# A perceiver block on one core: the pace of the gathers, the passage from the first mixture to cross-attention, and the order of five tiles

## The chip, the cores and the metric

The kernel runs as one program on one core of a Trainium2 chip. A core has five engines, each with an instruction queue of its own: TensorE (PE; its weight loads are listed apart as PEld), VectorE (DVE), ScalarE (ACT), GpSimd (POOL) and SyncE (SP, which here only issues DMAs). An engine works through its queue in order; where an instruction needs another engine's result, it waits on a semaphore, and everything behind it in that queue waits too. Transfers run on 16 DMA engines beside all this.

The metric is the device time of one execution in microseconds (us), as the median of several runs. All data are float32.

## The reference

Two layers over `x` of shape (16, 64, 256), that is 1024 tokens, with a context of 1601 rows of 256 for each of the 16 batches. Each step adds to `x`:

```python
    x = x + _L0_xattn_ref(ctx_1024, ctx_1024, _layernorm(x, axis=-1), mask_BxS2_if0, ...)
    x = x + _L0_attn_ref(_layernorm(x, axis=-1), ...)
    x = x + _L0_ffn_ref(_layernorm(x, axis=-1), ...)
    x = x + _L1_xattn_ref(_layernorm(x, axis=-1), ctx_1024, ...)
    x = x + _L1_attn_ref(_layernorm(x, axis=-1), ...)
    x = x + _L1_ffn_ref(_layernorm(x, axis=-1), ...)
    return x
```

- Layer 0, deformable attention: every query computes 5 sample positions for each of 16 heads from itself; at each position the keys and values of two neighbouring context rows are gathered and mixed, and a softmax over the 5 samples weighs them.
- Layer 0, attention: within a batch's 64 tokens, with normed queries and keys and a sigmoid instead of a softmax.
- Layer 0, mixture: 8 experts of width 512 with gelu gates, the best 2 per token.
- Layer 1, cross-attention: 16 heads of 64 over the context, 77 text rows and 1524 image rows with a softmax each, the two results added.
- Layer 1, state space: a convolution of 4 taps, then a recurrence over 64 tokens with 16 states, gated by a silu.
- Layer 1, mixture: 32 experts of width 128, the best 4 per token, and a shared expert of width 512.

## The kernel before

**Tiles and stages.** The 1024 tokens are 8 tiles of 128 (two batches each), held in `x4`. The work runs in this order:

1. *Keys and values* (`keys_values`, 113 steps `s`): context rows are loaded (`cx`), transposed on TensorE, multiplied by `wkv`, copied by ScalarE into `kv` and written to a table `tab` in DRAM for each tile of queries. Beside it DVE computes the sample positions, and `texts` prepares the text rows for cross-attention.
2. *Gathers and attends.* The sampled rows are fetched from the tables by `gather(k)`: DVE copies ten indices (`ig`), GpSimd issues ten indirect DMAs of 128 rows each (L446). Two gathers make a unit of four heads of one tile, and `attend(i)` (three pieces: DVE, one Exp on ScalarE, DVE) turns it into a part of `cv`. There are 32 units, four per tile, 64 gathers.
3. *Layer 0's rest for tiles 0 to 2* (`ND0 = 3`): `attention`, then `middle`, the mixture with all 8 experts computed on all tokens; the weights of an expert are three tiles of 512 KB in the tag `w` with four buffers. For tile 3 there is `attention` alone (`late`).
4. *Cross-attention* (`Cross`), 128 steps `n` (16 batches by 8 pairs of heads). A step multiplies the transposed context rows `cT` by the folded query `qf` (24 products `st`), takes a maximum on DVE (`mp`, `xmx`), subtracts it and exponentiates (`pt`), and one step later multiplies by the rows themselves (`cn`, L1096).
5. *Layer 0's rest for tiles 3 to 7*, beside cross-attention: `attention` and `middle` with a table `tb0`, which only route; then `slots` (which token stands in which block), `gelus` (17 blocks of 128 gathered tokens, each with one expert) and `combine` (the results gathered back, `yk`).
6. *State space and the second routing* beside the rest of cross-attention, and the second mixture at the end (`dense`, `Blocks`), beside the state space of the last two tiles.

**What sets the order.** The order on PE, DVE and ACT is the program's own (`manual_schedule`): generators yield pieces, and the loops place them. Gathers and attends are placed by `tick(us)`: it advances a clock of the program's own, by an amount in us that the program states for each piece of work, and issues a gather if `APART` (16.0; `APART_X`, 12.0, once `cr` exists) of it have passed since the last one and fewer than four units are open, and a piece of an attend if `AFTER` (42.0) have passed since its second gather. Nothing in it is measured at run time. GpSimd's queue holds the gathers and the memsets (`qbd`, `pt`, the column of ones in `cn`) in the order in which they are issued.

**The places that the change touches.**

- `tick`, L1551: the pace of the gathers.
- `mid`, L1579, called once in each step `s` from 60 on: one piece of `mids`, that is of `attention` or `middle` for tiles 0 to 2. `mids[0]` waits in the program's order until enough units are attended.
- From L1613: behind the keys and values, the loop `while mids`, which runs what is left of these pieces with no other work beside it; before it `qbd` gets its memset on GpSimd (L1619).
- `Cross.begin`, L1204: the first queries (`queries`, three parts; their weights `wq` are two loads of 512 KB), the turn of the context rows of batch 0 (`turn`), the loads for batch 1, the text part of batch 0, the first fold. `fold(n + 1)` at L1160 computes the next step's `qf`.
- From L1646: the side work of stage 5 as one chain, tile 3 singly, then 4 and 5, then 6 and 7 in pairs. `cr.step(side, side, side, side)` takes one piece of it at four places of a step, and `next(side, None)` a fifth. It must be done by `cr.n = 42`; what is left is run at once (`drain(side)`).
- `Blocks.fetch`, L1436, and `Blocks.down`, L1464: a block's weights are loaded for the expert whose number SP reads from `ev4`, which DVE copies (L1452); each block's result `yb` is copied out of PSUM by DVE and ScalarE in turn (`copy(n, ...)`).

## Time and profile before

| what | value |
|---|---|
| median of 3 runs | 3019.71 us (3013.13 to 3023.61) |
| the profiled execution | 3017.05 us, span from first to last instruction 3014.8 us |
| granted TensorE clock, mean | 0.974 |
| PE busy | 2826.2 us (94%), 17734 instructions |
| PEld busy | 2354.7 us (78%) |
| DVE busy | 1618.4 us (54%) |
| ACT busy | 1033.6 us (34%) |
| POOL busy | 819.7 us (27%), of it the gathers' indirect DMAs 613.2 us (640 of 958 ns) |
| HBM | 235.79 MB read, 74.62 MB written, 103 GB/s over the span |

The spans count from the first instruction. A group's idle time is that of its engine just ahead of the group's instructions, with what ended it; for an engine that isn't the bottleneck it costs nothing. Float32 products appear as two records each in the trace, so 9751 instructions of PE in the program are 17734 records. The granted clock is the share of full speed that the chip allows TensorE in a window; a busy time at a clock of 0.84 holds 0.84 of the work that the same busy time holds at full clock.

The page's 40 slices show in which stages PE is not full (tenths of each slice of 75 us; the PE clock and the share of the DMA engines below it):

```profile
PE   8999999967999998889979999999999999998699
DVE  3332133244666675553236766577544676655756
POOL 0655545556676730000010110011000020001623
PEclk9999999988999998899989999999999999999999
DMA  7666856636122221125521111122011021004853
```

The low digits of PE stand in four places: the first slice, slices 9 and 10 (600 to 750 us, the way from the keys and values to cross-attention), slices 16 to 18 and 21 (1125 to 1350 us and about 1500 us, tiles 3 to 7), and slices 37 and 38 (2700 to 2850 us, the start of the second mixture). GpSimd's digits of 5 to 7 between 75 and 1125 us are the gathers.

### The profile page before, as it was taken

The page shows a single profiled execution, that of the slowest core. Times are in us where ns is not written, and L with a number is a line of the kernel's source. Part 1 is how long each engine was busy: PE and PEld are TensorE (multiplying, and loading weights), DVE is VectorE, ACT ScalarE, POOL GpSimd, SP SyncE. Part 2 cuts the span into 40 slices and gives each one's busy share as a digit, 9 for nine tenths or more (in the row PEclk, how much of TensorE's full clock was granted, in tenths as well). Part 3 has the DMA queues.
Part 4 walks back from the last instruction along what each step waited for, and adds up shares of the span by engine and source line. Part 5 has one row for each costly group of instructions (what it writes and reads, how often), then busy time and mean ns, then how long its engine had stood idle before and what let it go on. Part 6 is the DMA issues. An engine that isn't in the chain of part 4 may idle for free.

```text
span 3014.8 us, 46081 instructions
## 1 busy us (share of the span) xinstructions
PE 2826.2 (94%) x17734; PEld 2354.7 (78%) x17734; DVE 1618.4 (54%) x4134; ACT 1033.6 (34%) x2375; POOL 819.7 (27%) x923
## 2 busy tenths in 40 slices
PE   8999999967999998889979999999999999998699
PEld 4554446656898997689969999899999999995587
DVE  3332133244666675553236766577544676655756
ACT  3433444323223223324323333343232443222431
POOL 0655545556676730000010110011000020001623
PEclk9999999988999998899989999999999999999999
DMA  7666856636122221125521111122011021004853
GB/s 231 177 194 213 252 167 179 196 110 189 34 64 56 71 56 48 36 96 182 188 68 55 60 60 55 35 75 70 17 47 58 29 88 62 8 1 128 242 150 112
DMA packets 324291, 313.43 MB, mean 104 GB/s; under 512 B 57941, under 2 KB 275321, under 8 KB 323561
## 3 DMA queue, kind: packets, MB, share of 16 engines
q1 hardware_dynamic: 171577, 212.52, 22.1%
q10 hardware_dynamic: 126928, 63.06, 7.3%
q0 software_dynamic: 25568, 34.91, 5.4%
q8 instruction: 141, 2.31, 0.3%
q14 instruction: 77, 0.63, 0.1%
HBM read 235.79 MB, written 74.62 MB: 103 GB/s over the span
## 4 chain that ended last, share of the span: by engine, by line
PE 82%; DVE 8%; DMA 4%; ACT 3%; issue 1%; POOL 0%; ACTq 0%; SPq 0%; DVEq 0%; POOLq 0%
PE st L88 35%; PE mm L1096 21%; PE mm L88 16%; PE mm L153 5%; PE mm L1052 2%; PE mm L1082 1%; DVE hs L1337 1%; DVE mp L1127 1%; PE mm L1021 1%; DMA w<-in_gate 1%; DMA wd<-in_down1T 1%; PE mm L1146 1%; DMA yk<-y0d,sli 1%; POOL g L446 0%; ACT pt L1168 0%
## 5 line engine op out<-in xcount | busy, mean ns | idle before, releaser
L1096 PE MATMUL mm<-cn,pt 128*128 128x257 f32 (+1 forms) x3072 | 745.0, 386 | 0.5 <-ACT cT L82 0.5
L88 PE MATMUL st<-qf,cT 128*128 128x128 f32 x6144 | 740.6, 278 | 0.9 <-ACT qf L1055 0.9
L446 POOL DMA_INDIRECT g<-tab,ig x640 | 613.2, 958 | 467.6 <-DVE ig L444 183.7
L88 PEld LDWEIGHTS st<-qf,cT 128*128 128x128 f32 x6144 | 722.2, 194 | 5.5 <-ACT qf L1055 1.7
L1096 PEld LDWEIGHTS mm<-cn,pt 128*128 128x128 f32 (+1 forms) x3072 | 557.1, 191 | 84.1 <-ACT cT L82 0.9
L88 PE MATMUL st<-wkv,cxt 128*128 128x512 f32 (+1 forms) x832 | 378.1, 599 | 2.8 <-ACT cxt L415 2.8
L1127 DVE TENSOR_REDUCE mp<-st 128x128 f32<-128x512 f32 x384 | 260.2, 686 | 208.4 <-PE st L88 208.1
L1167 DVE TENSOR_TENSOR pt<-st,mc 128x512 f32<-128x512 f32 (+1 forms) x384 | 224.0, 638 | 153.7 <-ACT mc L1158 153.7
L88 PEld LDWEIGHTS st<-wkv,cxt 128*128 128x128 f32 (+1 forms) x832 | 150.2, 189 | 160.7 <-issue 157.0
L1168 ACT ACTIVATE pt<-pt 128x512 f32<-128x512 f32 (+1 forms) x384 | 208.0, 588 | 50.3 <-DVE pt L1167 50.1
L399 ACT COPY kv<-st 128x512 f32<-128x512 f32 (+1 forms) x208 | 121.5, 586 | 199.9 <-PE st L88 198.8
L1158 ACT COPY mc<-mm 128x128 f32<-128x128 f32 x128 | 33.9, 265 | 394.2 <-PE mm L1156 393.7
L1105 ACT COPY ot<-mm 128x256 f32<-128x256 f32 x128 | 47.5, 371 | 336.1 <-PE mm L153 336.1
L957 POOL MEMSET cn<- 128x12 f32 x16 | 1.9, 122 | 522.0 <-PE mm L1096 512.2
L1443 POOL DMA_INDIRECT xb<-xnd,row x55 | 58.4, 1062 | 290.1 <-PE mm L1082 218.2
L1148 DVE TENSOR_REDUCE xmx<-mm 128x1 f32<-128x128 f32 x128 | 37.3, 291 | 186.1 <-PE mm L1146 186.1
L1343 POOL TENSOR_TENSOR mn<-mn,hc 128x512 f32<-128x512 f32 x64 | 82.0, 1281 | 169.4 <-DVE hc L1342 164.5
L1072 ACT COPY yt<-mm 128x64 f32<-128x64 f32 x128 | 27.2, 212 | 253.8 <-PE mm L88 253.8
L88 PE MATMUL mm<-xt,w 128*128 128x256 f32 (+1 forms) x512 | 98.5, 348 | 6.9 <-DMA w<-in_gate 5.2
L88 PEld LDWEIGHTS mm<-xt,w 128*128 128x128 f32 x512 | 86.4, 210 | 23.3 <-issue 9.6
L153 PEld LDWEIGHTS mm<-ident,cx 128*128 128x128 f32 (+1 forms) x416 | 52.9, 145 | 40.8 <-issue 28.5
L1337 DVE TENSOR_TENSOR_SCAN hs<-da,db 128x512 f32<-128x512 f32 x64 | 80.1, 1252 | 6.9 <-DVE db L1335 0.5
(466 smaller groups left out, 3884.0 us busy)
## 6 DMA issues: line engine op xcount, KB each, us to landing
tab<-kv ACTq DMA_DIRECT2D x48, 1024.0 KB
w<-in_gate SPq DMA_DIRECT2D x66, 512.0 KB
cx<-in_ctx SPq DMA_DIRECT2D x48, 512.0 KB
cn<-in_ctx SPq DMA_DIRECT2D x16, 1408.0 KB
w<-in_lin SPq DMA_DIRECT2D x33, 512.0 KB
wk<-in_xwkiT SPq DMA_DIRECT2D x32, 512.0 KB
wg<-in_guT SPq DMA_DIRECT2D x55, 256.0 KB
g<-tab,ig POOLq DMA_INDIRECT x640
```

The costliest lines, as they stand in the source:

```text
L88: nc.tensor.matmul(o, lhsT=l, rhs=r, start=i == 0, stop=i == len(pairs) - 1)
L153: nc.tensor.transpose(t[:ncol, i, :rows], b, ident[:rows, :rows])
L399: nc.scalar.copy(kv[:w, :, c, :], pk[:w].rearrange("p (h e) -> p h e", h=H0))
L446: nc.gpsimd.indirect_dma_start(out=gf[:, (half * n + s) * 4 * HD0 : (half * n + s + 1) * 4 * HD0], out_offset=None, in_=tables[j], in_offs ...
L1052: nc.tensor.matmul(pf[:, k * P : (k + 1) * P], lhsT=w[:, hp % 4, k * P : (k + 1) * P], rhs=rhs, start=True, stop=True)
L1096: nc.tensor.matmul(po, lhsT=pt[:w, c, :], rhs=cn[:w, c, :], start=c == 0, stop=c == NCH - 1)
L1127: nc.vector.tensor_reduce(mp_[:, i, :], s.rearrange("p c n -> p n c"), AX.X, ALU.max)
L1167: nc.vector.tensor_tensor(o, st[i][:, :m, :], mc.to_broadcast([P, m, P]), ALU.subtract)
L1168: nc.scalar.activation(o, o, AF.Exp)
L1337: nc.vector.tensor_tensor_scan(hs.rearrange("p c n -> p (c n)"), da.rearrange("p c n -> p (c n)"), db.rearrange("p c n -> p (c n)"), 0.0, ...
L1343: nc.gpsimd.tensor_tensor(y, y, hc, ALU.add)
L1443: nc.gpsimd.indirect_dma_start(out=x, out_offset=None, in_=xnd, in_offset=bass.IndirectOffsetOnAxis(ap=tb.row[:, i : i + 1], axis=0))
```

## The change

The gathers are 12.0 apart throughout. `mid` is called twice per step while `s < 94`. The first queries are placed between the last pieces of the mixture, with their weights in the mixture's own buffers `w`; `ahead` turns the context rows and folds steps 0 and 1 before the mixture's pool closes, and the text part of batch 0 goes into cross step 0. `fold` works two steps ahead, with a third buffer of `qf`, which moves to the pool `xc`. Tiles 3 to 7 are taken singly, in two rows with buffers of their own (`Row`; one buffer for each tag, `y` in that of `ct` and `sg` in that of `gt0`), one piece from each row by turns, and `slots` gives an empty piece after each of its own. In the second mixture the results of blocks with a number of `E1` or more are all copied by ScalarE, and the numbers of their experts are copied into `evs` in `slots`.

```diff
-APART, APART_X, AFTER = 16.0, 12.0, 42.0
+APART, AFTER = 12.0, 42.0
...
             nc.vector.tensor_copy(self.expert, pe[:1, : nb - b0])
+            self.evs = []
+            if self.own:
+                for q in range(0, nb - b0, 4):
+                    m = min(4, nb - b0 - q)
+                    self.evs.append(mk(rp, [1, 4], f"ev{q}", I32, bufs=1))
+                    nc.vector.tensor_copy(self.evs[-1][:, :m], self.expert[:, q : q + m])
...
+    class Row:
+
+        def __init__(self, pool, row):
+            self.pool, self.row = pool, row
+
+        def tile(self, shape, dtype, tag, name, bufs):
+            tag = {"y": "ct", "sg": "gt0"}.get(tag, tag)
+            return self.pool.tile(shape, dtype, tag=f"{tag}{self.row}", name=f"{name}{self.row}", bufs=bufs or 1)
+
-    def attention(t0, nt, lp, mw):
+    def attention(t0, nt, lp, mw, a0=0):
...
-        def queries(self, t, part):
+        def queries(self, t, part, pool=None):
...
+            tag, bufs = ("w", 4) if pool else ("wq", 2)
+            pool = pool or self.xp
...
-            qf = self.qf[n] = mk(self.xp, [P, KC, P], "qf", bufs=2)
+            qf = self.qf[n] = mk(self.xc, [P, KC, P], "qf", bufs=3)
...
-            self.fold(n + 1)
+            self.fold(n + 2)
...
+        def ahead(self, lp):
+
+            self.turn(0)
+            self.w[0, 0] = load(lp, "w", a["xwkiT"][:512, :].rearrange("(c p) d -> p c d", p=P), [P, 4, D], 4)
+            for n in range(2):
+                self.fold(n)
+
         def begin(self, xp):
+
             self.xp = xp
             self.text_loads(0)
             self.weights(0, 0)
-            yield
-            for part in range(3):
-                self.queries(0, part)
+            self.loads(1)
+
+            def pieces():
+                self.text(0, 0)
                 yield
-            self.turn(0)
-            self.loads(1)
-            yield
-            self.text(0, 0)
-            yield
-            self.text(0, 1)
-            self.text_turn(0, 0)
-            yield
-            self.text_turn(0, 1)
-            self.fold(0)
-            yield
+                self.text(0, 1)
+                self.text_turn(0, 0)
+                yield
+                self.text_turn(0, 1)
+                yield
+
+            return pieces()
...
-                    if r == 0:
-                        m = min(4, tb.nb - E1 - 4 * q)
-                        self.ev = mk(ep, [1, 4], "ev4", I32, bufs=3)
-                        nc.vector.tensor_copy(self.ev[:, :m], tb.expert[:, 4 * q : 4 * q + m])
-                    e = nc.sync.value_load(self.ev[0:1, r : r + 1], min_val=0, max_val=E1 - 1)
+                    e = nc.sync.value_load(tb.evs[q][0:1, r : r + 1], min_val=0, max_val=E1 - 1)
...
-            copy(n, self.y[:, self.m, :], po[:, :D])
+            copy(1 if i >= E1 else n, self.y[:, self.m, :], po[:, :D])
...
+    def taken_in_turns(gens):
+        while gens:
+            for z in list(gens):
+                if next(z, True) is None:
+                    yield
+                else:
+                    gens.remove(z)
+
+    def slower(gen):
+        for _ in gen:
+            yield
+            yield
...
-            pace["gather"] = now + (APART if cr is None else APART_X)
+            pace["gather"] = now + APART
...
             if lp:
                 mid()
+                if s < 94:
+                    mid()
...
+        i = 0
         while mids:
-            if attended() < mids[0][0]:
-                tick(2.4)
+            assert len(mids) == 1
+            if i in (3, 6):
+                cr.queries(0, i // 3 - 1, lp)
             mid()
+            i += 1
+        cr.queries(0, 2, lp)
         while attended() < 4 * (ND0 + 1):
             tick(2.4)
         drain(late)
+        cr.ahead(lp)
         slp.close()
...
-        drain(cr.begin(xp))
+        pieces = cr.begin(xp)
+        cr.step(pieces, pieces, None, pieces)
...
-        side = chain([middle(ND0, 1, lp, mw, tb0)]
-                     + [z for t0 in range(ND0 + 1, NPAIR, TG) for z in (attention(t0, TG, lp, mw), middle(t0, TG, lp, mw, tb0))]
-                     + [tb0.slots, lambda: gelus(lp, tb0), lambda: combine(lp, tb0, ND0, y0d, lambda t: None, 1)])
+        rows = [Row(lp, i) for i in range(TG)]
+        tiles = [[middle(ND0, 1, rows[0], mw, tb0)], []]
+        for t in range(ND0 + 1, NPAIR):
+            i = (t - ND0) % TG
+            tiles[i] += [attention(t, 1, rows[i], mw, i), middle(t, 1, rows[i], mw, tb0)]
+        side = chain([taken_in_turns([chain(z) for z in tiles]), lambda: slower(tb0.slots()),
+                      lambda: gelus(lp, tb0), lambda: combine(lp, tb0, ND0, y0d, lambda t: None, 1)])
```

More of the change, by code (lines that the diff above doesn't have):

```diff
@@ L768, in attention @@
                 nc.vector.tensor_scalar(sg[r], ps[r, r], 1.0 / math.sqrt(D), -math.log(S), ALU.mult, ALU.add)
-                nc.scalar.activation(att[t][r, r], sg[r], AF.Sigmoid)
+                nc.scalar.activation(att[a0 + t][r, r], sg[r], AF.Sigmoid)
         yield
@@ L777, in attention @@
                     lhsT=qkv[:, t, 2 * D + e * P : 2 * D + (e + 1) * P],
-                    rhs=att[t], start=True, stop=True,
+                    rhs=att[a0 + t], start=True, stop=True,
                 )
@@ L992, in turn @@
                 nc.scalar.copy(ct[:, k, IMG:], ct[:, k, : NCH * P - IMG])
-        def queries(self, t, part):
+        def queries(self, t, part, pool=None):
             if t >= NPAIR:
                 return
+            tag, bufs = ("w", 4) if pool else ("wq", 2)
+            pool = pool or self.xp
             if part == 0:
-                self.xn[t] = normed([t], "q", self.xp)
+                self.xn[t] = normed([t], "q", pool)
             elif part == 1:
-                self.xn[t] = turned(self.xn[t], 1, "q", self.xp)
+                self.xn[t] = turned(self.xn[t], 1, "q", pool)
             else:
@@ L1005, in queries @@
                 for q4 in range(2):
-                    w = load(self.xp, "wq", a["xwq4"][q4].rearrange("k c p n -> p (k c) n"), [P, 4, D], 2)
+                    w = load(pool, tag, a["xwq4"][q4].rearrange("k c p n -> p (k c) n"), [P, 4, D], bufs)
                     pq = bank().rearrange("p (c n) -> p c n", c=4)
```

## The prediction

> **What bounds the kernel now.** I first read the windows of the trace, cut where the program changes stage (columns: window; its length; busy us and instructions of PE, PEld, DVE, ACT, POOL; granted clock; DMA share; GB/s).
>
> ```profile
> 0.00:589.80 589.80, 567.89 (x1923) 315.97 (x1924) 181.07 (x592) 246.31 (x466) 283.01 (x310) 0.99 0.67 199
> 589.80:762.50 172.70, 119.66 (x623) 101.86 (x622) 77.07 (x240) 55.85 (x110) 104.75 (x112) 0.84 0.53 156
> 762.50:1134.00 371.50, 363.39 (x2697) 333.35 (x2697) 252.97 (x648) 101.68 (x269) 233.41 (x248) 0.99 0.23 58
> 1134.00:1305.30 171.30, 143.20 (x891) 125.90 (x892) 96.08 (x328) 61.69 (x140) 0.12 (x1) 0.88 0.10 33
> 1305.30:1489.70 184.40, 175.10 (x1294) 162.89 (x1294) 61.62 (x154) 62.78 (x135) 15.28 (x17) 0.98 0.54 172
> 1489.70:1541.50 51.80, 33.70 (x243) 30.80 (x243) 13.06 (x31) 10.54 (x24) 11.44 (x17) 0.86 0.36 112
> 1541.50:2724.00 1182.50, 1176.62 (x8753) 1080.72 (x8752) 743.91 (x1675) 407.87 (x992) 67.79 (x108) 1.00 0.16 48
> 2724.00:3014.80 290.80, 246.60 (x1316) 203.23 (x1316) 192.62 (x469) 86.84 (x240) 103.91 (x111) 0.97 0.56 164
> ```
>
> TensorE is the bound almost everywhere, so the time to win is what a stage is longer than its TensorE work at full clock, estimated as length minus busy times clock: 172.7 - 119.7 x 0.84 = 72 us in stage 2 (the end of layer 0 behind the keys and values), 45, 13 and 23 us in stages 4 to 6 (tiles 3 to 7 beside cross-attention: attention and routing, expert blocks, the last of both), 52 us in stage 8 (the second mixture), and 6 to 28 us in each of the others. The waits of PE then say what ends the idle time, in stage 2 and in stage 4 (us in total, times, longest).
>
> ```profile
> PE mm L153 <- DVE qkv L103: 7.4, 2, 5.4
> PE mm L88 <- DMA wq<-in_xwq: 7.2, 1, 7.2
> PE mm L153 <- DVE cv L499: 6.2, 1, 6.2
> ```
> ```profile
> PE mm L153 <- DVE xn L103: 15.6, 4, 5.5
> PE mm L153 <- DVE qkv L103: 7.1, 2, 3.6
> PE mm L1146 <- DVE mp L1129: 5.7, 3, 2.7
> ```
>
> They are dependent chains (a norm, then its transpose), not a full engine: DVE is busy 45% and 56% there. Last I read GpSimd's timeline at the end of the keys and values, and the timelines of DVE and PE at the end of stage 6 (start, duration, instruction, idle before it).
>
> ```profile
> 595.00 0.94 POOL L446 DMA_INDIRECT g<-tab,ig  x1 [0.30 <-issue]
> 596.24 0.94 POOL L446 DMA_INDIRECT g<-tab,ig  x1 [0.30 <-issue]
> 597.23 1.80 POOL L1619 MEMSET qbd<- 128x2048 f32 x1
> ```
> ```profile
> 1537.95 0.48 DVE L702 SCALAR_TENSOR_TENSOR x<-yk,gk,x 128x256 f32<-128x256 f32 x1 [0.89 <-DMA yk<-y0d,sli]
> 1538.36 1.28 DVE L1127 TENSOR_REDUCE mp<-st 128x128 f32<-128x512 f32 x2
> ```
> ```profile
> 1540.95 0.47 PE L1146 MATMUL mm<-ident,mp 128*128 128x128 f32 x1 [17.18 <-DVE mp L1129]
> ```
>
> A gather's indirect DMAs start 1.25 us apart back to back, so one call of `gather` (ten) costs GpSimd 12.5 us. The memsets of `qbd` stand behind the gathers in the same queue. At the end of stage 6 the combination's ten gathered rows hold DVE, and PE waits 17.18 us behind them.
>
> **The change, part by part.** Counted in the built order of both kernels, TensorE's 9751 instructions stay; they only move. The sum is of waits.
>
> *Gathers 12 apart, two calls of `mid` per step.* In the order before, 13 of the 32 attends and 30 of the 64 gathers stand ahead of the end of the keys and values; in the order after, 23 and 52. Tiles 0 to 2 move with them: of stage 2's PE work (256 records of 128x128 at 3.57/32 = 0.112 us, about 230 of 128x256 at 0.217, the rest some 23 us; 102 us, which agrees with 119.7 x 0.84 = 101) only two experts of tile 2, the first queries, the turn of the context rows and two folds stay behind the last `wkv` product: 22 us. The 77 us that move go into a stage whose PE is 96% busy, so they lengthen it by 77 us and cost nothing net; their weights (25 MB) are as many bytes as before, and 144 MB by 762 us become 146 MB by some 740 us, at 197 GB/s, the rate of stage 1. With 10 us for waits in the denser stretch and 10 in the remainder, PE alone would reach the first cross product at 590 + 77 + 10 + 22 + 10 = 709 us instead of 762.5.
>
> *What is late next.* That is not when it will get there. GpSimd issues its first gather at 77.4 us; at 12 us of model time per 12.5 us of work it has no pause afterwards. In the changed order `qbd`'s memset stands behind 52 gathers, not 30: 77.4 + 52 x 12.5 = 727 us at the least, 733 with the mean of 12.3 us from a gather's first start to its last end plus 0.3 to the next, then 1.8 us of memset. ScalarE's first write to `qbd` (the queries' scaling, L1012) waits for that memset, and behind it on ScalarE stand the copies of `cT` and of `qf`, which PE needs for the first cross product. Before, that way took 762.5 - 748.7 = 13.8 us, of which the text's part (753.4 to 760.9) now goes into step 0: 6.3 us remain. The first cross product is at 733 + 1.8 + 6.3 = 741, 21.5 us earlier; the text's 3 us of PE come back in step 0. Gain 19 us; bounds: -15 (all 52 at the longest call's 13.0 + 0.3: 775, less the text) to 50 (were GpSimd not late: 709, less the text). I stay by the mean of the 64 calls.
>
> *Queries, loads and folds moved ahead.* The 7.2 us wait for `wq` goes: its two 512 KB loads now use the mixture's `w` buffers and stand in SP's queue behind the last expert loads, with the slack until 733 above them. Were GpSimd not late, they would cost up to that 7.2 again. One more 512 KB load (`xwkiT`) and the earlier `cn` load for batch 1 lie in the same slack. `fold` two ahead removes two waits of 0.5 us.
>
> *Tiles 3 to 7 in two rows.* The last attend now stands at cross step 14 instead of 27, so the side work starts there. It has 122 pieces instead of 90, five per step: attention and routing at steps 14 to 23 (before 27 to 32), slots to 28, expert blocks at 29 to 35, combination at 36 to 38, all under the limit of 42; before, the last blocks and the whole combination were run at once between steps 41 and 42. One tile's norm is half the DVE work of two, and each row has two gaps to finish in, some 5 us of cross PE work instead of 2.5. A row has one buffer per tag, and `y` shares that of `ct`; its pieces follow each other anyway, so that costs nothing while they are two gaps apart. So of stage 4's 45 us I keep 12 (a gap between the third and fifth call is only the last product, 1.7 us); stage 5's 13 become 13, since 2.5 blocks per step stay; of stage 6's 23 I keep 8, because ten row gathers at 1.9 us each still pass DVE within two steps. Gain 33 + 15 = 48; bounds 15 (below) and 70 (all but the blocks' 13).
>
> The price is on ScalarE: 28 more table loads (112 to 140), 1.283 us each by the trace's rows, 36 us, of which about 14 loads, 18 us, fall on these ten steps. A step lasts some 15.7 us there, ScalarE's own work is 62 us in the 171 us of stage 4, so they hide unless one stands ahead of `mc` (L1158), whose copy frees the banks; a load on that way at every second step would cost 5 x 1.3 = 7 us.
>
> [...]
>
> *Copies on ScalarE, expert numbers ahead of the stage.* In stage 8 they take twelve copies from DVE and move six more away:
>
> ```profile
> L84 DVE COPY yb<-mm 128x256 f32<-128x256 f32 x12 | 5.0, 420 | 1.6 <-PE mm L88 1.6
> ...
> L1452 DVE COPY ev<-evr 1x4 int32<-1x4 int32 (+1 forms) x6 | 3.9, 648 | 0.0
> ```
>
> That is 8.9 us of DVE, which is on the chain from 2759 to 2793 and by turns with loads of `wd` (5 to 7.6 us each) until 2857. I take half, 5 us; bounds 0 and 10.
>
> Sum: 19 + 48 + 5 = 72 us, from a profiled span of 3014.8 us (3017.1 with what lies around it). The median of the three runs is 3019.7, 2.7 us above that execution; I take the 72 from the median: 2947.8, say 2947.
>
> **The rivals.** *TensorE sets the pace up to cross-attention*, GpSimd is not late: 31 us more, 2916. For it speaks that PE's own work ends at 709; against it 520 DMAs at 1.25 us, a pace that no row undercuts. 0.08.
>
> *The rows gain little*: DVE's queue, not the tile's chain, is what PE waits for (`mp` L1129 is in the list above), and more small norms and table loads leave it so. Then 15 of the 48 remain: 2980. For it: a step's own DVE work is 7 us of 12.3, and the order puts a second row's pieces between. Against it: stage 7 has DVE 63% busy and PE at 1176.6 of 1182.5. 0.15.
>
> *The gathers slow each other and the change is slower*: ScalarE waits for `qbd` behind all 52, so the start of cross-attention goes with 520 times one DMA. It turns at 762.5 + 50 = 812.5 us, that is at 1.40 us each instead of 1.25; at 1.45 us the first cross product is at 840, 77 us late, and 77 - 50 = 27 us are lost: 3047. For it: single DMAs of 1.42 us instead of 0.94 do occur (589.5). Against it: the ten take 12.2 to 13.0 us in all 64 calls, also where DVE is 68% busy (stage 3). 0.05.
>
> [...]
>
> *The parts cancel or the order doesn't bind*, about 3018: 0.02.
>
> **How the numbers follow.** Forecast 0.70, with its own range 2920 to 2972; rivals 0.08, 0.15, 0.05, 0.02. The time is the forecast's. The range takes in the first two rivals: 2905 to 2985. Faster by over 0.3% (9 us, about what a measurement here can tell): 0.70 + 0.08 + 0.15 = 0.93; within: 0.02; slower: 0.05.
>
> **What would show it.** After: back-to-back gathers from 77 us with no pause, `qbd`'s memset at 727 to 740 us, and ScalarE's first `qbd` write idle until then. Right also: no wait of 17 us of PE on `mp`, `xn` and `qkv` waits under 8 us together, clock above 0.95 in the side steps. Wrong: the memset reached before 715, the first cross product after 765, or a stage from the last attend to step 42 with more than 50 us between its length and its PE work.

## The result, and the profile after

| | before | after |
|---|---|---|
| median | 3021.66 us (3013.13 to 3027.21, 4 runs) | 2978.70 us (2978.07 to 2980.21, 4 runs) |
| span of the profiled execution | 3014.8 us | 2976.4 us |
| granted TensorE clock, mean | 0.974 | 0.980 |
| first score product `st` of cross-attention | 762.5 us | 754.8 us |
| cross steps 1 / 14 / 42 / 127 (start of `xmx`) | 782.5 / 955.5 / 1541.5 / 2719.5 | 781.4 / 956.5 / 1505.3 / 2677.3 |

The ratio is 0.9863, 95% interval 0.9842 to 0.9885: 43 us faster by the medians, 38.4 by the two spans. The forecast was 72. By the steps of cross-attention, which exist in both kernels, the 38.4 us fall as follows: -1.0 up to step 14 (forecast: 19), 37.2 from step 14 to 42 (48), 6.0 from 42 to 127 (nothing), -3.8 from the last step to the end (5). A step is marked by its maximum `xmx` on VectorE; the steps' times in this text are read from those instructions' starts in the trace. The last stretch, from the last `xmx` to the end, is 295.3 us before and 299.1 after (the prediction's last window begins 4.5 us behind the last `xmx`).

The windows of the changed kernel, cut where its stages change (columns as in the prediction: window; length; busy us and instructions of PE, PEld, DVE, ACT, POOL; granted clock; DMA share; GB/s):

```profile
0.00:590.00 590.00, 548.46 (x1936) 323.38 (x1936) 245.16 (x786) 243.60 (x462) 387.26 (x413) 0.98 0.65 192
590.00:754.80 164.80, 132.97 (x588) 89.44 (x588) 54.38 (x168) 65.24 (x124) 126.50 (x132) 0.90 0.66 194
754.80:956.50 201.70, 189.46 (x1424) 174.57 (x1424) 133.56 (x340) 57.68 (x144) 114.26 (x124) 0.98 0.27 68
956.50:1155.70 199.20, 177.60 (x1186) 159.41 (x1183) 115.10 (x359) 90.90 (x194) 0.12 (x1) 0.93 0.11 33
1155.70:1227.20 71.50, 70.40 (x521) 64.47 (x520) 37.85 (x122) 20.48 (x48) 2.04 (x3) 0.98 0.17 54
1227.20:1422.00 194.80, 191.31 (x1423) 178.24 (x1422) 60.08 (x138) 72.80 (x153) 15.61 (x18) 1.00 0.58 182
1422.00:1505.30 83.30, 83.30 (x621) 76.50 (x620) 48.25 (x113) 32.75 (x73) 9.54 (x17) 1.00 0.25 71
1505.30:2677.30 1172.00, 1167.65 (x8714) 1073.36 (x8714) 736.45 (x1657) 397.80 (x974) 67.58 (x107) 1.00 0.16 47
2677.30:2976.40 299.10, 250.10 (x1333) 205.53 (x1332) 195.57 (x457) 90.44 (x255) 107.45 (x111) 0.95 0.55 159
```

Row 4 is attention and routing of tiles 3 to 7, row 5 the slots, row 6 the expert blocks, row 7 the combination. Length minus busy times clock, the prediction's measure, is 199.2 - 177.6 x 0.93 = 34 us in row 4, 2.5 in row 5, 3.5 in row 6 and nothing in row 7, where the 17 us wait on `mp` stood before. So the later parts are better than forecast, and the attention steps keep 34 us where 12 were meant to stay.

**The front.** GpSimd's timeline of the changed kernel where the gathers meet the fill of `qbd`, then ScalarE's at the same place (start, duration, instruction, idle before it and what ended it):

```profile
745.08 0.95 POOL L446 DMA_INDIRECT g<-tab,ig  x1 [0.31 <-issue]
746.06 1.80 POOL L1652 MEMSET qbd<- 128x2048 f32 x1
```
```profile
747.90 1.19 ACT L1029 ACTIVATE qbd<-mm 64x512 f32<-64x512 f32 x2 [17.36 <-POOL qbd L1652]
```

The fill stands right behind a gather, with no pause, and ScalarE had been idle for 17.4 us when it could write `qbd`. That is the mechanism of the forecast. Its date was 733 there; it is 746.1: the first gather began at 84 us, not 77.4, and the 52 gathers ahead took (746.1 - 84) / 52 = 12.73 us each, not 12.6. Add 1.8 us of fill and the 6.3 us of the way behind it: 754.2, and the first score product is at 754.8. What TensorE lost by it is less than ScalarE's idle time, as PE's timeline, and below it a line of VectorE's, show:

```profile
728.70 1.22 PE L88 MATMUL mm<-w,act 128*128 128x256 f32 x2 [8.98 <-DVE act L886]
730.92 1.22 PE L88 MATMUL mm<-w,act 128*128 128x256 f32 x2 [1.00 <-DVE act L886]
731.94 6.15 PE L88 MATMUL mm<-qt,w 128*128 128x128 f32 x32
737.92 0.60 PE L153 MATMUL mm<-ident,cn 128*128 128x128 f32 x4
749.15 4.49 PE L153 MATMUL mm<-ident,cn 128*128 128x128 f32 x20 [10.62 <-ACT qbd L1029]
```
```profile
725.61 0.83 DVE L466 TENSOR_TENSOR pr<-g,qp 128x640 f32<-128x640 f32 x1 [10.57 <-DMA g<-tab,ig]
```

The queries' products (`mm<-qt,w`) ended at 738.1, and from there PE waits 10.6 us for `qbd`. Without the fill the first score product would stand at some 744, an estimate from that wait. The gathers held PE once before, and not through the fill: VectorE waits 10.6 us for a gather's rows with an attend, the last expert's `act` stands behind it in VectorE's queue, and PE waits 9.0 us for `act`.

Then PE waits in cross step 0 (waits of PE from 755 to 785 us: us in total, times, longest):

```profile
PE mm L153 <- DVE pet L1048: 6.7, 2, 3.9
```

`pet` is the softmax of the text rows, the part moved into step 0. From step 0 to step 1 it takes 19.4 us (10.4 before), so 9 us came back where the forecast had 3 us of PE work. Step 1 is 1.1 us earlier than before, and nothing is left of the front's gain.

**The attention steps.** PE's waits from step 14 to step 24:

```profile
PE mm L153 <- DVE xn L103: 7.2, 2, 6.9
PE mm L153 <- DVE xrc L1194: 5.0, 2, 2.8
PE mm L790 <- ACT att L784: 4.8, 2, 2.6
PE mm L1163 <- DVE mp L1146: 4.3, 2, 2.5
```

and a piece of the chain of waits there, in order of time (start, us, what):

```profile
1069.84 0.28 ACT mc L1175
1070.11 0.02 issue
1070.13 0.70 DVE pt L1184
1070.84 0.02 issue
1070.86 1.64 ACT pt L1185 x3
1072.50 0.20 ACT pt L1188
1072.70 0.02 issue
1072.72 1.28 ACT L99
1074.00 0.01 issue
1074.01 0.21 ACT sd L99
1074.22 0.02 issue
1074.25 0.17 DVE rs L101
1074.42 0.03 issue
1074.45 0.41 DVE xn L103
...
1075.00 0.66 PE mm L153 x2
```

One norm's root (`sd`, 0.21 us) waits on ScalarE behind three exponentials and a table load of 1.28 us (`ACT L99` without a name is the load); `xn` waits for it, PE's transposes wait for `xn`, and the products behind those wait too. The next exponentials, `pt` at 1092.3 us, have another load ahead of them, again 1.28 us. `mp`, DVE's own queue, ends 4.3 us of waits here.

### The profile page after: what moved, and what is told of

The parts are those of the page before. It is cut to its first block, busy times and chain, and to the rows that moved or that the text cites. A ratio compares the mean times of both kernels' runs of the same rounds, so it can differ in the third digit from the quotient of the medians.

```text
span 2976.4 us, 46295 instructions
## 1 busy us (share of the span) xinstructions
PE 2811.3 (94%) x17734; PEld 2344.9 (79%) x17734; DVE 1626.4 (55%) x4138; ACT 1071.7 (36%) x2427; POOL 830.4 (28%) x923
## 4 chain that ended last, share of the span: by engine, by line
PE 76%; DVE 8%; POOL 6%; issue 3%; DMA 3%; ACT 3%; SPq 1%; ACTq 0%; DVEq 0%; POOLq 0%
PE st L88 31%; PE mm L1113 21%; PE mm L88 14%; POOL g L446 6%; PE mm L153 4%; PE mm L1069 2%; DMA g<-tab,ig 2%; DVE hs L1359 1%; PE mm L1099 1%; DVE hc L1364 1%; PE mm L1038 1%; ACT pt L1185 1%; DVE db L1357 1%; DVE mp L1144 1%; PE mm L1163 1%
## 5 line engine op out<-in xcount | busy, mean ns | idle before, releaser
L446 POOL DMA_INDIRECT g<-tab,ig x640 | 620.2, 969 | 282.1 <-issue 176.9
L1347 POOL MEMSET da<- 128x8 f32 x64 | 7.5, 117 | 319.3 <-ACT da L1346 319.0
```

The lines of the kernel that those rows point to most:

```text
L446: nc.gpsimd.indirect_dma_start(out=gf[:, (half * n + s) * 4 * HD0 : (half * n + s + 1) * 4 * HD0], out_offset=None, in_=tables[j], in_offs ...
```

## The experiments

All twelve ran in later sessions, on chips where the same kernel before took 3278 to 3281 us, not 3021. In the kernel before (eighth run) 252 us of the difference lie ahead of step 14, 38 in steps 14 to 24, beside which the last gathers run, and 8 in the last stretch. In the first 590 us it moved 164 GB/s there and 199 in the first execution, and PE was 488 us busy instead of 568. The expectations call this slow memory, but the DMA engines were also less busy there, 0.54 of the time instead of 0.67, so they moved as much per busy share; why they stood idle, the traces don't show. From step 14 of the changed kernel on, things repeat closely: steps 14 to 42 took 548.8 us in the first execution and 548.7, 550.6, 548.7 and 548.2 in the four of these with the same side work (1, 4, 5 and 6), steps 42 to 127 took 1172.0 and 1171.9 to 1172.3. The front scatters (first score product of kernels with the same front: 984 to 1010 us), so the experiments are read by stage, and a median only together with the stage that the edit touches.

**1. The zero fill on VectorE.** Is it the fill behind the gathers that holds the front?

```diff
-            nc.gpsimd.memset(cn[:, :, D:], 1.0)
+            (nc.gpsimd if b else nc.vector).memset(cn[:, :, D:], 1.0)
...
-            nc.gpsimd.memset(qbds[i], 0.0)
+            nc.vector.memset(qbds[i], 0.0)
...
-            nc.gpsimd.memset(pts[i][:, CM, :], 0.0)
+            nc.vector.memset(pts[i][:, CM, :], 0.0)
```

> The changed kernel with the zero fills of `qbd` and `pt` (and the ones of `cn`, first batch) on VectorE instead of GpSimd. Theory A (the fill of `qbd`, queued on GpSimd behind 52 gathers, is what holds the front): ScalarE's first write into `qbd` comes at about 731 us (747.9 less the 17.4 us that it stood idle), the first score product at 737 to 745 us rather than 754.8, cross step 14 at 940 to 950 rather than 956.5, and the median falls by 8 to 16 us, to 2963-2971. Theory B (TensorE's own work and its waits for the mixture's activations end at the same time as the fill): the first score product stays at 751-755 us and the median at 2975-2982. Theory C: the front comes earlier, but the attends that ride on cross steps 0 to 14 then wait for the gathers, the last of which ends at 910 us: step 1 is early by 8 us or more, step 14 by less than 4, the median within 4 us of 2978.7.

Measured: 3292.63 us; first score product 1008.4 us, step 14 at 1253.0, against 1005.8 and 1248.4 in the fourth run and 1002.9 and 1240.7 in the fifth, with the fill on GpSimd. Inconclusive, as none of the three theories was put to the test: with this front the fill came at 968.8 us and ScalarE's first write into `qbd` at 996.6 (fifth run), so there was nothing for it to hold. That the fill held the first execution is read from its trace, above, and was not shown by an experiment.

**2. Pairs again.** How much of the 37 us is the early start, how much the two rows?

```diff
-        rows = [Row(lp, i) for i in range(TG)]
-        tiles = [[middle(ND0, 1, rows[0], mw, tb0)], []]
...
+        side = chain([middle(ND0, 1, lp, mw, tb0)]
+                     + [z for t0 in range(ND0 + 1, NPAIR, TG) for z in (attention(t0, TG, lp, mw), middle(t0, TG, lp, mw, tb0))]
+                     + [tb0.slots, lambda: gelus(lp, tb0), lambda: combine(lp, tb0, ND0, y0d, lambda t: None, 1)])
```

> The changed kernel with the old side chain for tiles 3 to 7: attention and middle of two tiles at a time, one chain, slots at full pace; the early start (cross step 14), the closer gathers and the copies stay. Theory A (most of the 37 us between steps 14 and 42 come from the early start, after which the chain rides on more cross steps, and two rows bring little because ScalarE's table loads and exponentials set the gaps): steps 14 to 42 take 555-565 us rather than 548.8 and the median rises by 6 to 16 us, to 2985-2995. Theory B (the two rows are the gain): steps 14 to 42 take 575-586 us and the median rises by 26 to 37 us, to 3005-3016. Theory C (two rows cost more in table loads than they hide): 540-548 us, the median 2970-2978.

Measured: 3305.94 us; steps 14 to 42 in 570.2 us, 21.5 more than the 548.7 of the first run on the same chip. Between A and B: the rows are worth some 21 us in these steps. Against the kernel before on that chip the median is slower, ratio 1.0093 (1.0054 to 1.0133).

**3. No change of table, the roots on VectorE.**

```diff
+    def inverse_root(o, v, n, eps):
...
+        nc.vector.tensor_scalar(h, v, eps, None, ALU.add)
+        nc.vector.tensor_scalar(o.bitcast(I32), h.bitcast(I32), -0.5, float(0x5F3759DF), ALU.mult, ALU.add)
+        for _ in range(3):
+            nc.vector.tensor_tensor(t, o, o, ALU.mult)
+            nc.vector.scalar_tensor_tensor(t, t, -0.5, h, ALU.mult, ALU.mult)
+            nc.vector.scalar_tensor_tensor(o, t, 1.5, o, ALU.add, ALU.mult)
...
-        nc.scalar.activation(sd, sd, AF.Sqrt)
...
+        if power:
+            inverse_root(rs, mv[:, :, 1], n, LN_EPS)
```

> The changed kernel with no change of ScalarE's table in the attention steps of tiles 3 to 7: the inverse roots of the norms are worked out on VectorE (a first guess from the bits, three Newton steps, 11 small instructions in place of an addition, a root on ScalarE and a reciprocal), the sigmoid as an exponential on ScalarE, an addition and a reciprocal on VectorE. What is computed stays the same up to rounding. Theory A (table loads of 1.28 us and the exponentials queued behind them set the gaps of cross steps 14 to 24, which take 199.2 us for 177.6 us of TensorE work): those steps take 178-189 us and the median falls by 10 to 21 us, to 2958-2969. Theory B (the gaps are the side chain's own length from engine to engine, whichever engine does the root): the steps take 194-203 us, the median is 2974-2983.

Measured: 3298.52 us; steps 14 to 24 in 213.0 us. Both theories missed: it is 14 us slower than the 199.0 beside it. The trace has each of the small instructions (128x1) at 0.17 us and the next 0.02 later, so eleven are 2.1 us on the path from the statistics to `xn`, more than the table load, root and reciprocal of the chain above (1.28 + 0.21 + 0.17 = 1.66), and they stand ahead of the cross steps' own `pt` in VectorE's queue, which is 145.7 us busy in these steps instead of 115.1. The loads were gone, but VectorE's work had grown by 30 us, so the run doesn't tell what the loads cost.

**4. The expert numbers back in `fetch`.**

```diff
-                    e = nc.sync.value_load(tb.evs[q][0:1, r : r + 1], min_val=0, max_val=E1 - 1)
+                    if r == 0:
+                        m = min(4, tb.nb - E1 - 4 * q)
+                        self.ev = mk(ep, [1, 4], "ev4", I32, bufs=3)
+                        nc.vector.tensor_copy(self.ev[:, :m], tb.expert[:, 4 * q : 4 * q + m])
+                    e = nc.sync.value_load(self.ev[0:1, r : r + 1], min_val=0, max_val=E1 - 1)
```

> The changed kernel with the six copies of expert numbers back in the blocks' fetch, as before the change; the `yb` copies stay on ScalarE. Theory A (with the numbers copied ahead, SyncE no longer stops for VectorE, and the blocks' weights go into the DMA queues ahead of the state-space rows, which makes `dt` land 48.9 us after the last `xmx` instead of 38.9): `dt` lands 37-41 us after the last `xmx`, the stretch from the last `xmx` to the end takes 290-294 us rather than 299.1, and the median falls by 5 to 9 us, to 2970-2974. Theory B (the `yb` copies on ScalarE, or nothing that repeats, make the stretch longer): it stays at 297-301 us and the median at 2976-2981.

Measured: 3284.00 us; VectorE's first use of `dt` 40.5 us after the last `xmx`, against 47.4 to 47.8 with the numbers ahead (first, second, third and fifth run) and 48.9 in the first execution. That is A for the delay. The last stretch took 309.7 us against 307.8 to 313.8, within the scatter, so its length doesn't decide.

**5 to 8, on one chip.** The changed kernel again; fill and expert numbers undone together; no change of table at no price elsewhere; the kernel before.

> The changed kernel once more, unchanged, as the measure for what is run beside it. If the memory is as fast as in the first execution (192 GB/s over the first 590 us), the median is 2975-2983 us, the first score product comes at 753-757 us and the last stretch, from the last `xmx` to the end, takes 297-301 us. If it is as slow as in the session of the first four experiments (146 GB/s there), the first score product comes at 1000-1010 us and the time is 3275-3300 us; cross steps 14 to 42 take 547-551 us in both.

Measured: 3269.76 us (3248.10 to 3284.67), the kernel before beside it 3278.19: ratio 0.9952, 0.9917 to 0.9987. The change gains less there. On the chip of the first four runs the changed kernel itself was not run; the first run, which differs from it in the fills alone, is slower than the kernel before (1.0040, 1.0008 to 1.0072), so there the change may gain nothing. First score product 1002.9, steps 14 to 42 548.7, last stretch 313.5 us.

> The changed kernel with two edits in stages far apart, each read from its own stage: the zero fills on VectorE, and the copies of expert numbers back in the blocks' fetch. Where memory is fast: theory A (the fill behind 52 gathers holds the front) puts the first score product at 737-745 us rather than 754.8 and step 14 at 940-950 rather than 956.5; theory B (TensorE and the mixture's end hold it anyway) at 751-756; theory C: the first score product 10 us earlier but step 14 within 4 us, because the attends then wait for gathers. For the last stretch, theory A (block weights ahead of the state-space rows) gives 290-294 us rather than 299.1 and `dt` 37-41 us after the last `xmx`, theory B 297-301. Both A: median 2955-2965. Where memory is slow, neither front can be told, and the last stretch is compared with that of the unchanged kernel beside it.

Measured: 3269.93 us; `dt` used 38.0 us after the last `xmx`, last stretch 304.0 us (first score product 1009.9: the front can't be told). SyncE's timeline behind the last `xmx`, first of the changed kernel (fifth run, last `xmx` at 2961.3), then of this one (2965.1):

```profile
2998.56 0.38 SPq L1444 DMA_DIRECT2D wg<-in_guT  x1
2999.13 0.34 SPq L1445 DMA_DIRECT2D wd<-in_down1T  x1
2999.69 0.38 SPq L1444 DMA_DIRECT2D wg<-in_guT  x1
3000.18 0.39 SPq L1302 DMA_DIRECT2D rows<-dt  x1
...
3004.31 0.33 SPq L1307 DMA_DIRECT2D dt<-rows  x1
```
```profile
2996.60 0.32 SPq L1302 DMA_DIRECT2D rows<-dt  x1
2998.54 0.33 SPq L1307 DMA_DIRECT2D dt<-rows  x1
...
3007.53 0.40 SPq L1444 DMA_DIRECT2D wg<-in_guT  x1
```

ScalarE had copied the rows' source by 31.6 us after the last `xmx` in both. With the numbers in `fetch` the rows leave at once, 31.5, and the blocks' weights (`in_guT`) stop for VectorE's copy until 42.4. With the numbers ahead the weights run from 23.7 on, and the rows leave at 38.9.

> The changed kernel without any change of ScalarE's table in the attention steps of tiles 3 to 7, at no cost to another engine: the square root of the norms in these steps is left out (the reciprocal is of the variance itself), and the sigmoid is a tanh, halved and shifted on VectorE, with the same result. Theory A (the table loads and what is queued behind them are what the steps lose; the version with roots on VectorE only lost it again to 11 instructions of 0.17 us in a row): steps 14 to 24 take 182-191 us rather than 199.2, steps 14 to 42 531-541, the median falls by 8 to 17 us against the unchanged one beside it. Theory B (the gaps are the chain from engine to engine and VectorE's queue): steps 14 to 24 take 194-200 us, and the median stays within 4 us.

```diff
-        nc.scalar.activation(sd, sd, AF.Sqrt)
+        if not rootless:
+            nc.scalar.activation(sd, sd, AF.Sqrt)
...
-                nc.scalar.activation(att[a0 + t][r, r], sg[r], AF.Sigmoid)
...
+                if rootless:
+                    nc.scalar.activation(sg[r], sg[r], AF.Tanh)
+                    nc.vector.tensor_scalar(att[a0 + t][r, r], sg[r], 0.5, 0.5, ALU.mult, ALU.add)
```

Measured: 3244.98 us; the kernel leaves out the norms' square root in these steps, so it shows a time and no usable result. The window of steps 14 to 24 in the changed kernel beside it, and in this one:

```profile
1240.70:1439.70 199.00, 176.72 (x1185) 158.45 (x1183) 115.14 (x358) 90.80 (x194) 0.12 (x1) 0.94 0.10 33
```
```profile
1222.00:1407.20 185.20, 170.41 (x1185) 151.41 (x1183) 116.47 (x366) 51.13 (x148) 0.12 (x1) 0.97 0.11 35
```

Theory A: 13.8 us shorter, with ScalarE 39.7 us less busy (the trace has 29 table loads in these steps in the changed kernel and none here), VectorE as busy as before and the clock at 0.97 instead of 0.94; steps 24 to 42 are the same, 349.7 us in both. Of the 35.0 us by which the two spans differ (3274.8 and 3239.8), 18.7 were there at step 14, ahead of the edit; these are the front's scatter.

> The kernel before, for a trace from the same chip as the three beside it. Where memory is fast: first score product at 760-765 us, step 14 at 953-958, the last stretch 294-297 us. Where memory is slow: theory A (the closer gathers take transfer time from the key and value products, so the changed kernel's front loses) puts the first score product at 960-990 us, 15 us or more ahead of the changed kernel's; theory B (the front is as late with either) within 8 us of the changed kernel's.

Measured: one run of 3313.4 us, above the median of its kernel (3278.19). The first score product comes at 930.5 us, 72 us ahead of the changed kernel's 1002.9, far over what A had put down; that it is transfer time that the gathers take is not shown by it, since the mixture's products too were moved into that stage. By step 14 33 us of the lead are left, and at step 42 the changed kernel is 40 us ahead (1829.4 against 1789.4): the attends still ride on the old kernel's steps, the last of them at step 27 (VectorE's last write to `cv`).

**9 and 10. A short root, and two ways to get the rows out.** Both kernels:

```diff
+        nc.vector.tensor_scalar(o.bitcast(I32), v.bitcast(I32), -0.5, SEED, ALU.mult, ALU.add)
+        nc.vector.tensor_tensor(w, o, o, ALU.mult)
+        nc.vector.scalar_tensor_tensor(w, v, eps, w, ALU.add, ALU.mult)
+        nc.vector.scalar_tensor_tensor(w, w, -K2 * 10.0 / 3.0, w, ALU.add, ALU.mult)
+        nc.vector.scalar_tensor_tensor(o, w, 5.0 * K2 * K2, o, ALU.add, ALU.mult)
```

The ninth also:

```diff
-            nc.sync.dma_start(out=rows, in_=prm)
+            q = nc.scalar if wide else nc.sync
+            q.dma_start(out=rows, in_=prm)
```

> The changed kernel with two edits in stages far apart. First, no change of ScalarE's table in the attention steps, at a smaller price than in the first trial: the inverse root as 5 VectorE instructions (a first guess from the bits and one step of third order, off by up to 0.0002), the sigmoid as a tanh. Second, the state-space rows of the last group go out and come back through ScalarE's DMA queue instead of SyncE's, so that the block weights can't stand ahead of them there. Theory A for the first (each instruction more than the 2 of the version without roots costs 3.1 us over the ten steps: 213.0 less 185.2 us over 9 instructions): steps 14 to 24 take 192-197 us; theory B (what counts is how long VectorE is held ahead of the exponentials, with a threshold): under 189 or over 199. For the second, theory A (SyncE's order is what made `dt` late): `dt` lands 37-42 us after the last `xmx` rather than 47-49 and the last stretch takes 298-305 us, against 308-314 with the unchanged queue; theory B (the weights hold the DMA engines, whichever queue `dt` stands in): 45-50 us, the last stretch 307-315.

Measured: 3260.39 us. Steps 14 to 24 in 190.8 us: just under A's range, above B's 189. For the rows B's numbers: `dt` used at 49.2, last stretch 313.0 us. But B's reason is not the main one: the rows left ScalarE's queue only at 38.5, though their source was ready at 31.6 and no block weight stands in that queue. The semaphores in the trace of the changed kernel's first execution say why: the 683 transfers of SyncE and ScalarE signal on the same eight, 85 or 86 on each, GpSimd's 746 on eight others, and ahead of 572 of the 683 stands a wait for the transfer's own semaphore. `rows` has the same one there as the eighth transfer before it, a `wd` issued at 2710.53 us. That `wd` landed at 2716.26, SyncE's wait for the semaphore ended at 2716.34, and the rows left at 2716.39, though ScalarE had copied their source by 2708.84. So the weights hold the rows whichever of the two queues these stand in (38.9 us on SyncE's, 38.5 on ScalarE's). ScalarE's own work stood behind the rows as well: its next `sl` had been held for 16.0 us.

> The changed kernel with the short inverse root and tanh in the attention steps, and the copies of expert numbers back in the blocks' fetch. Steps 14 to 24 as in the kernel run beside it, within 2 us. `dt` lands 38-41 us after the last `xmx`, and the last stretch takes 303-310 us (304.0 and 309.7 in the two runs with this edit). If both repeat, the median is 8 to 14 us below the 3269.8 us of the changed kernel in this kind of session: 3256-3262.

Measured: 3245.74 us (3244.15 to 3253.07), ratio 0.9875, 0.9809 to 0.9941; steps 14 to 24 in 192.5 us, `dt` used at 38.0, last stretch 305.3 us. All as expected but the median, which is 10 us below the range: step 14 was 16 us earlier than in the fifth run, which is the front.

**11. Gathers 15 apart.**

```diff
-APART, AFTER = 12.0, 42.0
+APART, AFTER = 15.0, 42.0
```

> The changed kernel with the gathers spaced at 15 us of modelled time instead of 12, before and in the cross steps. In a session of slow memory: theory A (the closer gathers take transfer time from the key and value products' rows, and that is why the changed kernel reaches step 14 at 1240.7 us and the kernel before at 1207.4): the first score product comes 15 us or more before 1003 and step 14 at or before 1225. Theory B (the mixture that now runs inside the key and value stage, with its weights, makes the front as long as it is; the spacing is no matter): first score product and step 14 within 10 us of 1003 and 1241. Theory C (the closer gathers pay): step 14 at 1255 or later, as the last attends wait for their gathers.

Measured: 3315.65 us, ratio 1.0090 (1.0058 to 1.0121): slower than the kernel before. First score product at 898.4 and step 14 at 1197.0, which are A's numbers, and yet it loses: the last attend is at step 25, the side work begins there, and what isn't done of it at step 42 is run at once, 138.9 us from step 41 to 42 (51.7 in the kernel before). Step 42 is at 1827.3.

**12. The rows on GpSimd's queue**, with the short root and the numbers ahead, for the two causes that the ninth run had left:

```diff
-            nc.sync.dma_start(out=rows, in_=prm)
+            q = nc.gpsimd if wide else nc.sync
+            q.dma_start(out=rows, in_=prm)
```

> The changed kernel with the short inverse root and tanh in the attention steps, the copies of expert numbers left ahead as the change has them, and the state-space rows of the last group on GpSimd's DMA queue. In the list of instructions every transfer that SyncE or ScalarE issues takes one of eight semaphores by turns and waits until the eighth transfer before it has landed; GpSimd's transfers have eight of their own. Theory A (that turn is what holds the rows: on SyncE's queue they left 38.9 us after the last `xmx`, on ScalarE's 38.5, though `dt` had been copied at 31.6): the rows leave at 31.5-34 us, `dt` lands at 36-42, with the block weights still from 23.6 us on, and the last stretch takes 296-304 us. Theory B (the weights fill the DMA engines): the rows leave by 34 us, but `dt` lands at 45-50 and the last stretch takes 307-314. Steps 14 to 24 take 190-193 us, as in the two runs before.

Measured: 3254.28 us, ratio 0.9912 (0.9885 to 0.9939). GpSimd's timeline, the last `xmx` at 2947.8:

```profile
2979.62 0.58 POOL L1328 DMA_DIRECT2D rows<-dt  x1 [4.58 <-ACT dt L1326]
2986.04 0.59 POOL L1333 DMA_DIRECT2D dt<-rows  x1 [5.84 <-DMA rows<-dt]
```

The rows leave 31.8 us after the last `xmx`, as soon as they are copied: A. But they take 6.4 us until `dt` can follow (4.1 in the fifth run, 1.9 in the sixth), and `dt` is used at 44.0: between A and B. The last stretch is 306.8 us. So the turn of the semaphores is the larger part of the delay: of the 10 us between the fifth and the sixth run, the rows leave 7.3 later and take 2.2 longer. Whether the 6.4 here are the weights' traffic or GpSimd's own queue, no run separates.

## Why the prediction was partly right

Direction and range hold (2978.70 in 2905 to 2985); the gain is 43 us of the 72, which lands near the rival "the rows gain little" (2980) by luck: that rival named VectorE's queue, `mp` ends only 4.3 us of waits in the attention steps, and the rows gained most of what was forecast. Of the signs, three came (no 17 us wait on `mp`, `xn` and `qkv` at 7.2 us together, no stage with 50 us of gaps); the clock in the attention steps, 0.93, stayed under 0.95.

- **Front, 19 us forecast, -1.0 by step 14.** "Back-to-back gathers", "`qbd`'s memset stands behind 52 gathers" and ScalarE idle until then are all in the trace. The sizes failed: "77.4 + 52 x 12.6" was 84 + 52 x 12.73, 13 us later (the memset at 746.1, outside the 727 to 740 of the list), and "the text's 3 us of PE come back in step 0" was 9 us. The step priced PE's work, and what came back was a chain, the text's softmax on VectorE and ScalarE, with PE waiting. The sum for PE alone, 709, was off too: the last `wkv` product ended at 696.7 instead of 677 (590 + 77 + 10), and without the fill PE would still have come to the first score product at some 744, by the wait of 10.6 us.
- **Rows, 48 us forecast, 37.2.** "I keep 12" of stage 4, which no sum in the prediction yields, became 34; "13 become 13" and "I keep 8" became 6 and nothing. The step that failed is "so they hide unless one stands ahead of `mc`": the table loads stand ahead of the norms' roots as well, and those are on PE's path. The seventh run takes them away and wins 13.8 us. By the same measure 20 us of gaps stay there (185.2 - 170.4 x 0.97), against 33 in the fifth run, so the loads explain the larger part of the miss; what holds the other 8 us above the 12 was not tried. ScalarE's share in these steps (91 of 199 us busy) had made them look free.
- **Early start.** It was right that the gathers' pace matters, but not only for the first cross product. The eleventh run has an earlier front than the changed kernel and loses. At step 42 the kernel before stands at 1829.4 us, the rows with a late start at 1827.3, pairs with the early start at 1821.7, both together at 1789.4 to 1801.7 (four runs; these are different chips and a front that scatters). The closer gathers make room for 122 pieces, and the rows use it. The kernel before has only one trace here, of a run 35 us above its median; by the medians on their own chips either half alone is slower than the kernel before, 3305.94 to 3278.21 and 3315.65 to 3281.02. That the two halves need each other is what this suggests; how much each gives by itself isn't shown.
- **Steps 42 to 127, 6 us not forecast.** 1178.0, 1178.1 and 1178.4 us in the three runs whose side work ends at step 42 (before, twice, and the eleventh), 1170.4 to 1172.3 in the others, where it ends earlier, whether in rows or in pairs. What in it costs the 6 us was not tried.
- **Last stretch, 5 us forecast, -3.8.** The 8.9 us of copies left VectorE as priced, and yet it is as busy as before, 195.6 us against 195.2. Eight of the sixteen products `hc` take 1.58 us instead of 0.69, and these are the ones that start while GpSimd's addition `mn` is running, each with 1.03 us of it to go (GpSimd's line first, then VectorE's):

```profile
2769.12 1.57 POOL L1365 TENSOR_TENSOR mn<-mn,hc 128x512 f32<-128x512 f32 x1
```
```profile
2764.17 0.69 DVE L1364 TENSOR_TENSOR hc<-hs,pc 128x512 f32<-128x512 f32 x1
...
2769.66 1.58 DVE L1364 TENSOR_TENSOR hc<-hs,pc 128x512 f32<-128x512 f32 x1
```

  That is 7.1 us of the 8.9. It isn't what sets the stretch's length in the experiments: the first and the fifth run are without it and have the longest last stretches (in the fifth, VectorE is 190.0 us busy in 313.5). The step also forgot a queue that it moves past: without VectorE's copies SyncE no longer stops, the block weights go first, and `dt` is used 47.4 to 49.5 us after the last `xmx` instead of 38.0 to 40.5 (seven executions with numbers ahead and the rows on SyncE, against three of the changed kernel without them). On the experiments' chips the last stretches are 311.3 against 306.3 us, the means of six and of three, whose ranges overlap (307.8 to 313.8, 304.0 to 309.7). That part of the 9 us comes back because the weights are there sooner is a guess.

Of the rivals, TensorE at the pace (2916) is excluded by the memset's date and by PE's wait behind it, and the gathers did not slow each other: 12.2 to 13.0 us each in the first execution. In the chain above a change of table costs its load of 1.28 us and no more: the load starts 0.02 us behind the exponential, and `sd` 0.01 us behind the load. Open are what holds the front on the experiments' chips, why the change gains 8 us there by the medians (16 by the ratio) and 43 in the first session, and whether the fill on VectorE would win up to those 10.6 us where it is the fill that binds.

The tenth run is the version that beats both there: 3245.74 us (four runs), against 3281.02 for the kernel before on its own chip and 3269.76 for the changed kernel on another. By stage it wins 7.8 us in the attention steps (191.6, the mean of runs 9, 10 and 12, against 199.4, of runs 1, 4, 5 and 6) and some 5 in the last stretch; the rest is front.

## What to carry to other kernels

Work taken off one engine's queue let the block weights behind it go earlier here, and the rows left 38.9 us after the last `xmx` instead of 31.5: ask what will then stand ahead of the transfer that the critical chain needs, and whether the two share a semaphore, as `rows` and a `wd` do here. ScalarE, busy 91 of 199 us, still delayed a chain that passes it at each step, and without its table loads and roots the steps were 13.8 us shorter; count what a short instruction finds ahead of it there, table loads included (1.28 us each), not the engine's share. And price a moved piece by its chain from engine to engine, not by the bound engine's work in it: in cross step 0 it was 9 us instead of 3.

## What the runs showed of the hardware

Without the table loads (seventh run against the fifth), TensorE's gaps in steps 14 to 24 fell from 22.3 to 14.8 us, and its busy time for the same products from 176.7 to 170.4, at a granted clock of 0.97 instead of 0.94: 7.5 and 6.3 of the 13.8 us. Busy time times clock is 165 and 166 us. The same shows within the changed kernel's first execution: 32 products `st` took 3.74 us at 1117.9, 5.11 at 1075.5 and 6.11 at 1097.3, where the granted clock was 1.00, 0.72 and 0.59.

VectorE's product `hc` (128x512) took 1.58 us each of the eight times in the changed kernel's first execution that it started while GpSimd's addition `mn` was running. The other eight there, and the sixteen of the kernel before, none of which started so, took 0.69 to 0.71 us.

The same program took 3020 us in one session and 3280 in others. In the kernel before the difference lies up to step 24, where the last gather is issued, and in the last stretch; steps 24 to 127, bound by TensorE for the most part, agree within 2 us of 1625.
